# Splitting the transposes of an attention kernel's exponentials into halves of 64 rows

## The chip, the core and the metric

The kernel is one program on one core of a Trainium2 chip. The core has a matrix engine (TensorE, in the profile PE for its matmuls and PEld for the loads of the stationary operand, "weights"), a vector engine (DVE), a scalar engine (ACT), a general engine (GpSimd, POOL) and a queue engine (SP) which here issues DMA transfers. The engines run beside each other and meet at semaphores. Matmuls write into PSUM, eight banks of 128 partitions by 512 float32; DVE and ACT read it from there. The metric is the device time of one execution in microseconds (us); lower is better.

## What is computed

Two decoder layers over 8 sequences of 512 tokens of width 256, all in float32: an attention with relative positions, a feed-forward network with low-rank additions, a second attention, and a mixture of experts. The change lies in the first attention alone, 16 heads of width 16:

```python
scores = jnp.einsum('bhqd,bhkd->bhqk', q, k) / scale
c2p = jnp.take_along_axis(c2p_att, c2p_pos, axis=-1)
p2c = jnp.swapaxes(jnp.take_along_axis(p2c_att, p2c_pos, axis=-1), -1, -2)
scores = scores + (c2p + p2c) / scale
probs = jax.nn.softmax(scores, axis=-1)
ctx = jnp.einsum('bhqk,bhkd->bhqd', probs, v)
```

## The kernel before

The first attention is a loop of 256 steps. A step takes one block of 128 queries (i, one of 4) and two heads (p, one of 2, for the pair within a group of four heads, g) of one sequence (b). It works on the scores of 128 queries by 512 keys, once for each of the two heads. The order of the instructions on each engine is the order in which the program writes them (a schedule by hand); the semaphores are put in where tiles and PSUM banks are shared. What a step n issues, in this order:

- `products`, L363: matmuls of queries by keys into two score banks `sc` (one for each head; there are only two, so the last step's must have been read). Each uses 32 rows of the array. Between its parts stands `strips` for the step five ahead.
- `strips`, L306 to L343: matmuls of 32 rows (`pa`) with the position keys; ACT copies them to SBUF (L313), SP writes them to DRAM (`shift`) and reads them back a row shifted against the next (`winp`, `winc`), and POOL adds a correction (L316, L343). This is how the gather by relative position is made; it gives the DMA engines most of their work.
- `near_keys`, L375: 4 or 6 transposes of 128x128 from `winp`, added onto the score banks.
- `weights`, L389 and L391: DVE adds `winc` to a score bank, writes the result to SBUF as `e` and reduces it to a row bound `low`; ACT takes the exponential in place and sums it.
- `turned`, L394 to L402: the exponentials of the step before, two tiles `e` of 128 queries by 512 keys, are transposed so that keys lie on the partitions. For each tile four transposes of 128x128 fill one bank `et_ps` (L398), and DVE copies the bank to SBUF as `et` (L400). A transpose is a load of the block of `e` as weights, through which an identity streams. There are two such banks, and six tiles `et`.
- `weigh`, L410, in every odd step: 32 matmuls multiply four tiles `et` of two earlier steps by the values. Each loads 16 columns of values and streams 128 columns of `et`, into 32 columns of the array, one strip for each of four heads.
- at most one of a list of other jobs: a projection of queries or keys (`pq`, L282), values (`pv`, L270), the transposes of the normalizer (`spread`, L442), of the normalized input (`pt`, L264), or the output projection (`po`, L455), and with them layer norms on DVE and POOL.

The array is thus used in several shapes in turn: 32 rows (L363, L306), the whole (L375, L398, L282 and the other jobs), and strips of 32 columns (L410).

Of the kernel before, what the change touches and what calls it, by code (L numbers as in the profile page):

```python
# [12 lines left out]
F32 = mybir.dt.float32  # L13
# [8 lines left out]
P = 128  # L22
B, S, H = 8, 512, 256
NT = S // P
# [65 lines left out]
def _l0_attention(nc, tc, a, x, ident, mhalf, carry, prefetch):  # L90
# [6 lines left out]
    with ExitStack() as ctx:  # L97
# [5 lines left out]
        ps_t = pool("a_pst", 2, space=PSUM)  # L103
# [14 lines left out]
        with tc.tile_pool(name="a_pos", bufs=1) as pp:  # L118
# [62 lines left out]
            for n, c in enumerate((P - 1, 0)):  # L181
                f = pp.tile([P, NH, HD], F32, tag=f"end{n}", name=f"end{n}")
# [15 lines left out]
            for (w, name), e0 in (((wq, "bq"), HD), ((wk, "bk"), HD + 2)):  # L198
                for n, f in enumerate(ends):
                    e = e0 + n  # L200
# [8 lines left out]
            for n, (name, e) in enumerate((("bq", HD + 2), ("bq", HD + 3), ("bk", HD), ("bk", HD + 1))):  # L209
# [3 lines left out]
                for g in range(NG):  # L213
                    c = NG * n + g
# [11 lines left out]
        sb = pool("a_sb", 2)  # L226
# [25 lines left out]
        def later(steps, *fs):  # L252
            side.extend((now + steps, f) for f in fs)
# [13 lines left out]
        def values(b, t):  # L267
            pv = misc("pv")
            for k in range(NK):
                nc.tensor.matmul(  # L270
                    pv[:, :H], xnT[:, k, t * P : (t + 1) * P], wv[:, k, :], start=k == 0, stop=k == NK - 1
                )
            nc.vector.tensor_tensor(vs[b % 2][:, t, :], pv[:, :H], rows["bv"], ALU.add)

        def project(b, g):

            sm[b, g] = out = [sb.tile([P, S], F32, tag=f"sm{n}", name=f"sm{n}") for n in range(4)]

            def half(w, n, scale):
                pq = misc("pq")  # L280
                for k in range(NK):
                    nc.tensor.matmul(  # L282
                        pq,
                        w[:, k, 4 * g : 4 * g + 4, :].rearrange("p h e -> p (h e)"),
                        xnT[:, k, :],
                        start=k == 0,
                        stop=k == NK - 1,
                    )
                for m in (n, n + 1):
                    nc.scalar.activation(out[m], pq, AF.Identity, bias=bias[:, m, g : g + 1], scale=scale)  # L290

            return [partial(half, wq, 0, -SCALE), partial(half, wk, 2, 1.0)]
# [98 lines left out]
            nc.scalar.activation(e, e, AF.Exp, bias=low, scale=-1.0, accum_out=totals[b, g][:, i, r : r + 1])  # L391
            return e

        def turned(e):  # L394
            et_ps = ps_t.tile([P, S], F32, tag="pst", name="et_ps")
            for m in range(NT):
                ms = slice(m * P, (m + 1) * P)
                nc.tensor.transpose(et_ps[:, ms], e[:, ms], ident)  # L398
            et = sb.tile([P, S], F32, tag="et", name="et", bufs=6)
            nc.vector.tensor_copy(et, et_ps)  # L400
            return et

        def weigh(n, ets):

            b, g, i, _ = steps[n]
            v = vs[b % 2]
            for m in range(NT):
                for r, et in enumerate(ets):
                    h = 4 * g + r
                    nc.tensor.matmul(  # L410
                        ctx_ps[32 * r : 32 * r + HD, i * P : (i + 1) * P],
                        v[:, m, HD * h : HD * h + HD],
                        et[:, m * P : (m + 1) * P],
                        start=m == 0,
                        stop=m == NT - 1,
                        skip_group_check=True,
                    )
            if i < NT - 1:
                return
            c = sb.tile([P, S], F32, tag="c", name="c", bufs=2)  # L420
            nc.scalar.copy(c, ctx_ps)

            rec = sb.tile([P, NT, 4], F32, tag="rec", name="rec")
            nc.vector.reciprocal(rec, totals.pop((b, g)))
            wide = sb.tile([P, NT, P], F32, tag="wide", name="wide", bufs=1)
            nc.gpsimd.tensor_copy(
                wide.rearrange("p i (r e) -> p i r e", e=32), rec.unsqueeze(3).to_broadcast([P, NT, 4, 32])
            )
            later(3, partial(divide, b, c, wide))
            if g == NG - 1:  # L430
                out, measure, norm = finish(b)
                if b == B - 1:
                    rest.extend([*[partial(out, t) for t in range(NT)], measure, norm])
                else:
                    later(3, *[partial(out, t, misc, sb) for t in range(NT)])
                    later(9, partial(measure, misc, sb))
                    later(12, partial(norm, misc, sb))
# [9 lines left out]
        def finish(b):  # L447

            xn = xns[b % 2]
            stats = []  # L450

            def out(t, bank, pool):
                po = bank("po")
                for g in range(NG):
                    nc.tensor.matmul(  # L455
                        po[:, :H], cns[b][g][:, t * P : (t + 1) * P], wo[:, g, :], start=g == 0, stop=g == NG - 1
                    )
                nc.vector.tensor_tensor(xn[:, t, :], xn[:, t, :], po[:, :H], ALU.add)
                nc.gpsimd.tensor_tensor(xn[:, t, :], xn[:, t, :], rows["bo"], ALU.add)

            def measure(bank, pool):
                stats.extend(_batch_norm_stats(nc, pool, [xn[:, t, :] for t in range(NT)], 1e-7, mhalf))

            def norm(bank, pool):
                for t in range(NT):
                    _normalize(nc, xn[:, t, :], xn[:, t, :], *stats, t)
                    nc.gpsimd.tensor_tensor(xn[:, t, :], xn[:, t, :], rows["ln_scale"], ALU.mult)
                    nc.gpsimd.tensor_tensor(xn[:, t, :], xn[:, t, :], rows["ln_bias"], ALU.add)
                    nc.gpsimd.tensor_tensor(x[b][:, t, :], x[b][:, t, :], xn[:, t, :], ALU.add)

            return out, measure, norm
# [6 lines left out]
        with tc.manual_schedule():  # L478
            for f in [partial(turn, 0, k) for k in range(NK)] + project(0, 0):
                f()  # L480
            for u in range(AHEAD):
                strips(u)
                if u:
                    values(0, u - 1)
            es, ets = None, deque()
            for now in range(len(steps) + 3):
                n = now
                if n < len(steps):
                    b, g, i, p = steps[n]
                    if (i, p) == (0, 0):  # L490
                        totals[b, g] = sb.tile([P, NT, 4], F32, tag="totals", name="totals", bufs=3)
                        if g in (0, NG - 1):
                            while side:
                                side.popleft()[1]()
                        if g + 1 < NG:
                            urgent.extend(project(b, g + 1))
                        elif b + 1 < B:
                            urgent.extend(project(b + 1, 0))
                            later(0, *[partial(values, b + 1, t) for t in range(NT)])
                        if g == NG - 2 and b + 1 < B:  # L500
                            measure, norm = normalized(sb, b + 1)
                            later(1, measure)
                            later(3, norm, *[partial(turn, b + 1, k) for k in range(NK)])
                    scs, parts = products(n)
                    parts.pop(0)()
                    more = parts.pop() if parts else None
                    if n + AHEAD < len(steps):
                        strips(n + AHEAD, more)
                    else:
                        if more is not None:  # L510
                            more()
                        for todo in (reads, adds):
                            if todo:
                                todo.pop(0)()
                    new = []
                    for j in range(2):
                        near_keys(n, j, scs[j])
                        new.append(weights(n, j, scs[j]))
                if n <= len(steps):
                    if es:  # L520
                        ets.extend(turned(e) for e in es)
                    es = new
                if n % 2 and len(ets) >= 4:
                    weigh(n - 3, [ets.popleft() for _ in range(4)])
                if urgent:
                    urgent.popleft()()
                elif side and side[0][0] <= n:
                    side.popleft()[1]()
                for f in prefetch.get(n - len(steps), ()):
                    f(misc, sb)  # L530
            while side:
                side.popleft()[1]()
# [1128 lines left out]
```

## Time and profile before

| What | Value |
|---|---|
| median of 3 runs | 2162.43 us (2162.23 to 2166.1) |
| the profiled execution | 2158.92 us, span 2157.1 us |
| mean granted TensorE clock | 0.962 of full |
| stretch 54 to 600 us: PE, DVE, ACT, POOL busy | 533.5, 378.9, 377.1, 366.0 us; clock 0.99; DMA 0.90, 280 GB/s |
| stretch 600 to 1100 us: the same | 489.3, 347.6, 343.3, 345.9 us; clock 1.00; DMA 0.89, 277 GB/s |
| first and last transpose of L398 | 63.1 and 1149.7 us |
| L398 PEld, weight loads | 2048, 142 ns each, 232.6 us |
| L306 PE / L363 PE / L375 PE busy | 301.6 / 323.0 / 199.7 us |
| L410 PE | 4096, 274 ns each, 137.2 us busy |
| L391 ACT | 512, 716 ns each, 365.9 us |

The span runs from the first instruction to the last and is 1.8 us shorter than the execution's time. "Busy" for PE is the union of pipelined records: a matmul of 273 ns may start every 109, so a busy PE is not one at its peak, and distances between starts tell more than durations. A row of a group gives line, engine, operation, tile written and read, shapes and count; then the busy time in us and the mean in ns of one; then the idle time of the engine just before it and what ended most of it. A row of the timeline gives start and length in us; several like instructions are merged into one row with their count. A row of waits gives who waited for whom, the sum in us, the number of times and the longest.

### The profile page before, as it was taken

The numbers are of one execution on the slowest core, as the hardware profiler recorded it, in microseconds if no ns is written. First come the engines' busy times: TensorE is split into PE (matmuls) and PEld (weight loads), VectorE is DVE, ScalarE is ACT, GpSimd is POOL, SyncE is SP. The second block draws the span as 40 slices with busy tenths as digits, with TensorE's granted clock in tenths as the row PEclk, the third lists the DMA queues.
The fourth block names the chain that finished last, engine by engine and source line by source line (L and its number), as shares of the span: only waits on it lengthen the run. The fifth ranks groups of instructions, "written<-read, shape, count | busy, mean of one in ns | idle before, by whom it ended". The sixth has DMA issues, their size and how long they took to land.

```text
span 2157.1 us, 46358 instructions
## 1 busy us (share of the span) xinstructions
PE 1989.8 (92%) x16100; PEld 1439.5 (67%) x16100; DVE 1401.4 (65%) x3716; ACT 1112.0 (52%) x2382; POOL 1140.5 (53%) x1342
## 2 busy tenths in 40 slices
PE   7999999999999999999998999989988877499997
PEld 4777777777777777767775666645554445388886
DVE  2576676766767677676776655337887776356666
ACT  2776666676666767667662211244444423144443
POOL 4666766767667667676673210112544544355555
PEclk7999999999999999999999999999999987699999
DMA  8998888898898988889893344900111113656888
GB/s 271 317 295 274 273 277 275 277 291 259 265 284 256 296 265 278 281 266 291 266 303 107 100 148 140 122 18 11 46 41 39 51 44 112 248 164 204 260 261 266
DMA packets 389175, 444.50 MB, mean 206 GB/s; under 512 B 43345, under 2 KB 368209, under 8 KB 388945
## 3 DMA queue, kind: packets, MB, share of 16 engines
q1 hardware_dynamic: 374160, 402.20, 61.7%
q0 software_dynamic: 13824, 38.29, 4.8%
q8 instruction: 132, 2.16, 0.4%
q10 hardware_dynamic: 960, 1.05, 0.2%
q14 instruction: 99, 0.80, 0.1%
HBM read 239.26 MB, written 202.19 MB: 205 GB/s over the span
## 4 chain that ended last, share of the span: by engine, by line
PE 27%; DVE 10%; issue 4%; POOL 4%; DMA 3%; ACT 2%; POOLq 0%; DVEq 0%; ACTq 0%; SPq 0%
PE po L665 5%; PE pge L1421 4%; PE ph L657 3%; POOL results L860 2%; PE poe L1439 2%; PE pq L916 2%; PE ao L1006 1%; DVE prod L777 1%; PE po L1035 1%; PE pv L928 1%; DVE value L777 1%; PE ps L953 1%; DVE st L52 1%; DVE xn L62 1%; PE ptr L1413 1%
## 5 line engine op out<-in xcount | busy, mean ns | idle before, releaser
L389 DVE CUSTOM_DVE_ANT_0 e<-sc,winc 128x512 f32<-128x512 f32 x512 | 333.3, 688 | 294.9 <-PE sc L375 133.6
L391 ACT ACTIVATE e<-e,low 128x512 f32<-128x512 f32 x512 | 365.9, 716 | 111.2 <-DVE low L389 105.9
L313 ACT COPY strip<-pa 128x512 f32<-128x512 f32 x512 | 275.3, 591 | 212.7 <-issue 81.3
L316 POOL TENSOR_TENSOR own<-aside,strip 128x512 f32<-128x512 f32 x256 | 268.5, 1049 | 217.5 <-ACT strip L313 198.7
L363 PE MATMUL sc<-sm,sm 32*128 32x256 f32 (+3 forms) x1792 | 323.0, 440 | 15.4 <-DVE low L389 15.4
L400 DVE COPY et<-et_ps 128x512 f32<-128x512 f32 x512 | 328.5, 683 | 0.3 <-PE et_ps L398 0.2
L306 PE MATMUL pa<-pos,sm 32*128 32x256 f32 x2048 | 301.6, 408 | 2.3 <-ACT strip L313 1.3
L398 PE MATMUL et_ps<-ident,e 128*128 128x128 f32 x2048 | 266.4, 273 | 0.2 <-DVE et L400 0.2
L860 POOL DMA_INDIRECT rows<-pay,slot x128 | 141.6, 1106 | 229.5 <-issue 216.3
L363 PEld LDWEIGHTS sc<-sm,sm 32*128 32x128 f32 x1792 | 162.3, 184 | 124.6 <-issue 49.6
L398 PEld LDWEIGHTS et_ps<-ident,e 128*128 128x128 f32 x2048 | 232.6, 142 | 0.6 <-ACT e L391 0.5
L343 POOL TENSOR_TENSOR winp<-winp,own 128x256 f32<-128x256 f32 x256 | 186.5, 728 | 74.8 <-DMA winp<-shift 63.7
L860 POOL DMA_INDIRECT results<-y,r x160 | 155.8, 974 | 122.1 <-ACT y L1441 74.7
L375 PE MATMUL sc<-ident,winp 128*128 128x128 f32 x1280 | 199.7, 285 | 5.3 <-DMA winp<-shift 5.0
L343 POOL TENSOR_TENSOR winc<-winc,own 128x256 f32<-128x256 f32 x256 | 186.6, 729 | 34.1 <-DMA winc<-shift 31.0
L306 PEld LDWEIGHTS pa<-pos,sm 32*128 32x128 f32 x2048 | 180.9, 188 | 15.0 <-ACT strip L313 4.7
L375 PEld LDWEIGHTS sc<-ident,winp 128*128 128x128 f32 x1280 | 136.3, 141 | 81.4 <-issue 63.2
L57 POOL TENSOR_TENSOR rstd<-var,mhalf 128x4 f32<-128x4 f32 x40 | 44.8, 1121 | 252.6 <-DVE var L55 230.6
L1421 PE MATMUL pge<-store,rT 128*128 x640 | 167.9, 385 | 1.1 <-DVE rT L1415 0.5
L410 PE MATMUL ctx_ps<-et,v 128*16 128x128 f32 x4096 | 137.2, 274 | 0.2 <-DVE et L400 0.2
L660 ACT ACTIVATE hT<-ph,b 128x512 f32<-128x512 f32 x64 | 44.0, 687 | 169.8 <-PE ph L657 169.8
L282 PE MATMUL pq<-xnT,wqk 128*128 128x512 f32 x256 | 126.1, 614 | 3.6 <-DVE xnT L77 3.6
(216 smaller groups left out, 3421.4 us busy)
## 6 DMA issues: line engine op xcount, KB each, us to landing
shift<-strip SPq DMA_DIRECT2D x256, 510.0 KB
winp<-shift SPq DMA_DIRECT2D x128, 384.0 KB
winc<-shift SPq DMA_DIRECT2D x128, 384.0 KB
winp<-shift SPq DMA_DIRECT2D x128, 256.0 KB
winc<-shift SPq DMA_DIRECT2D x128, 256.0 KB
rows<-empty SPq DMA_DIRECT2D x8, 2640.0 KB
r<-rows SPq DMA_DIRECT2D x160, 132.0 KB
z<-results SPq DMA_DIRECT2D x32, 512.0 KB
```

Of the source, the lines that this page charges most:

```text
L306: nc.tensor.matmul(pa[:, t * W : (t + 1) * W], src[rs, i * P : (i + 1) * P], pos[rs, g, :], start=True, stop=True)
L313: nc.scalar.copy(st[:, 2 * j : 2 * j + 2, :].rearrange("p t w -> p (t w)"), pas[j])
L316: nc.gpsimd.tensor_tensor(own, aside.unsqueeze(2).to_broadcast([P, 2, 2, P]), st[:, :, W - 1 : W].rearrange("p (j t) o -> p t j o", t=2).t ...
L343: nc.gpsimd.tensor_tensor(dst, dst, own[:, t], ALU.add)
L363: nc.tensor.matmul(sc[:, c0:c1], s[side_][rs, cut : cut + P], s[2 + side_][rs, c0:c1], start=c0 == 0, stop=False, skip_group_check=True,)
L375: nc.tensor.matmul(sc[:, m * P : (m + 1) * P], wins[n + 2 * (m - i)][1][:, j, (i - m + 1) * P : (i - m + 2) * P], ident, start=False, stop ...
L389: nc.vector.tensor_tensor_reduce(e, sc, wins[n][0][:, j, :], 1.0, -LOW, ALU.add, ALU.min, low)
L391: nc.scalar.activation(e, e, AF.Exp, bias=low, scale=-1.0, accum_out=totals[b, g][:, i, r : r + 1])
L398: nc.tensor.transpose(et_ps[:, ms], e[:, ms], ident)
L400: nc.vector.tensor_copy(et, et_ps)
L860: ins = nc.gpsimd.indirect_dma_start(to, bass.IndirectOffsetOnAxis(ap=index, axis=0), source, None, bounds_check=last)
L1421: nc.tensor.matmul(pg[:, :H], rT[:, k * P : (k + 1) * P], w[:, k * H : (k + 1) * H], start=k == 0, stop=k == NK - 1)
```

## The change

Each transpose of a 128x128 block of `e` becomes two: one of the rows 0 to 63 of the array (queries 0 to 63), one of the rows 64 to 127. Each loads a block of 64 rows by 128 columns as weights and streams the 64 columns of the matching quarter of the identity. All blocks of the first half, of both heads, go into one bank and those of the second half into the other. DVE copies each bank into a half of one larger tile `et`, of which there are three in place of six small ones. The weighing streams its 128 columns as two runs of 64 from the two halves.

```diff
-        def turned(e):
-            et_ps = ps_t.tile([P, S], F32, tag="pst", name="et_ps")
-            for m in range(NT):
-                ms = slice(m * P, (m + 1) * P)
-                nc.tensor.transpose(et_ps[:, ms], e[:, ms], ident)
-            et = sb.tile([P, S], F32, tag="et", name="et", bufs=6)
-            nc.vector.tensor_copy(et, et_ps)
-            return et
+        def turned(es):
+            banks = [ps_t.tile([P, S], F32, tag="pst", name="et_ps") for _ in range(2)]
+            for j, e in enumerate(es):
+                for m in range(NT):
+                    for f, bank in enumerate(banks):
+                        rs, c = slice(64 * f, 64 * f + 64), (j * NT + m) * 64
+                        nc.tensor.transpose(bank[:, c : c + 64], e[rs, m * P : (m + 1) * P], ident[rs, rs])
+            et = sb.tile([P, 2, 2, NT, 64], F32, tag="et", name="et", bufs=3)
+            for f, bank in enumerate(banks):
+                nc.vector.tensor_copy(et[:, f].rearrange("p j m q -> p (j m q)"), bank)
+            return [et[:, :, j] for j in range(2)]
...
-                        et[:, m * P : (m + 1) * P],
+                        et[:, :, m, :],
...
-                        ets.extend(turned(e) for e in es)
+                        ets.extend(turned(es))
```

Nothing else is changed: the order of the jobs, the number of copies and of matmuls of every other line are the same.

## The prediction

> **What bounds the kernel now.** I read the page first, for where TensorE is nearly full; then the list of waits over 100 to 1100 us, for who makes it stop; then the timeline of single steps, for what each batch of instructions costs.
>
> ```profile
> PE 1989.8 (92%) x16100; PEld 1439.5 (67%) x16100; DVE 1401.4 (65%) x3716; ACT 1112.0 (52%) x2382; POOL 1140.5 (53%) x1342
> ...
> L389 DVE CUSTOM_DVE_ANT_0 e<-sc,winc 128x512 f32<-128x512 f32 x512 | 333.3, 688 | 294.9 <-PE sc L375 133.6
> ...
> L400 DVE COPY et<-et_ps 128x512 f32<-128x512 f32 x512 | 328.5, 683 | 0.3 <-PE et_ps L398 0.2
> ...
> L398 PE MATMUL et_ps<-ident,e 128*128 128x128 f32 x2048 | 266.4, 273 | 0.2 <-DVE et L400 0.2
> ```
>
> The transposes (L398) run from 63 to 1150 us: 8 in each of 256 steps. The loop takes 4.27 us a step over its steady part. VectorE, ACT and POOL each have idle time there; the waits say what TensorE stops for:
>
> ```profile
> PEld sc L363 <- DVE low L389: 37.8, 96, 1.1
> PEld sc L363 <- DVE et L400: 29.1, 56, 0.8
> ...
> PEld sc L375 <- DMA winp<-shift: 4.2, 9, 0.8
> ```
>
> TensorE stops about once in two steps, at the start of a step (L363), until VectorE has reduced the last score bank (L389) and so freed it. In all other steps it is TensorE's own work that sets the step. Two steps in a row, one without the weighing (L410) and one with it:
>
> ```profile
> 427.25 0.66 PE L375 MATMUL sc<-ident,winp 128*128 128x128 f32 x4
> 427.74 1.04 PE L398 MATMUL et_ps<-ident,e 128*128 128x128 f32 x8
> 428.61 1.88 PE L282 MATMUL pq<-xnT,wqk 128*128 128x512 f32 x4
> ...
> 431.50 0.66 PE L375 MATMUL sc<-ident,winp 128*128 128x128 f32 x4
> 431.99 1.04 PE L398 MATMUL et_ps<-ident,e 128*128 128x128 f32 x8
> 432.96 1.07 PE L410 MATMUL ctx_ps<-et,v 128*16 128x128 f32 x32
> ```
>
> Eight transposes last 1.04 us with a tail of 0.27, so one starts every (1.04-0.27)/7 = 0.11 us. Counted from first weight load to the next group's first load, the group takes 0.87 us when a full-array matmul follows (L282) and 1.07 when the array's shape changes after it (L410, L363): a change of shape costs 0.20 us, of which 0.11 is the last matmul's own streaming and 0.09 a drain.
>
> **What one split transpose costs.** The price depends on whether a block of 128x128 is held up by its weights (a block of e, 128 columns) or by what streams (the identity, 128 columns before, 64 after). Where the shape has just changed, the trace shows the two apart:
>
> ```profile
> 403.19 0.14 PEld L375 LDWEIGHTS sc<-ident,winp 128*128 128x128 f32 x1 [0.33 <-issue]
> ...
> 403.25 0.14 PEld L375 LDWEIGHTS sc<-ident,winp 128*128 128x128 f32 x1
> ...
> 403.36 0.38 PE L375 MATMUL sc<-ident,winp 128*128 128x128 f32 x2
> ```
>
> The second load can begin when the first matmul takes the first set of weights over: 0.06 us. The second matmul follows 0.11 us later. So in a transpose loading takes 60 ns, streaming 128 columns 109, and the load is hidden behind the streaming of the one before. Halving the columns leaves 54 ns of streaming, and 60 ns of loading becomes the limit.
>
> Here two rules of the Trainium skill speak against the change. Its page "TensorE: Matmul & The Clock Gate", section "LDWEIGHTS (loading the stationary operand)", prices a load by columns alone, 128/1.2 = 107 ns, whatever the rows. Then a split block still needs 107 ns and nothing is won. The trace agrees for ordinary loads (two of one row group start at 402.11 and 402.22) but shows 60 for the load of a transpose; I take 60. The same page, section "Part 3: Packing small matmuls", says that a load overlaps matmuls in flight only if their row groups differ: then a row group needs 60+54 = 114 ns a block. The trace has all 128 rows loading while all 128 stream (the next L375 load starts within 2 ns of the matmul before it), so I take max(60,54) = 60.
>
> Whether the two halves run side by side isn't in the trace for 64 rows. The nearest row is four groups of 32 rows:
>
> ```profile
> 402.11 0.19 PEld L363 LDWEIGHTS sc<-sm,sm 32*128 32x128 f32 x2 [0.76 <-issue]
> 402.12 0.19 PEld L306 LDWEIGHTS pa<-pos,sm 32*128 32x128 f32 x2
> ```
>
> Four loads of 0.19 us start within 20 ns, and their matmuls write four banks at once, 7 ns apart. The two halves likewise have disjoint rows and one bank each. Bounds for a block: 54 (only streaming counts) to 120 ns (halves take turns, 2x60). I take 60, plus 7 once for the second half.
>
> **The sum for a step.** New: a change of shape between L375 and the transposes, 0.20. The transposes: 8x0.060 + 0.054 for the last streaming + 0.007 + 0.09 drain = 0.63. Together 0.83 in place of 1.07 or 0.87. So a weighing step gains 0.24 us, a step whose transposes precede a full-array matmul 0.04.
>
> The other edits: VectorE still makes two 128x512 copies of 683 ns a step, now each a half of the queries; the layout of et moves in SBUF, capacity stays 6x512 columns, and L410 streams the same 128 columns as two runs of 64: nothing (no strided stream is in the loop to price it; if it cost 10% it would be 0.1 us per weighing, half the gain). The first copy now waits for all transposes rather than four, but on VectorE it stands behind the two reductions (L389), which end about 1.7 us after the last weight load of L375, when the transposes (0.2+0.6) are over: hidden. The first transposes need both banks free: in the trace the second copy is done at least 0.30 us before the next step's first transpose: hidden. PE issues 16 loads and matmuls more a step, at 7 ns each 0.11 of the 0.6: hidden. No DMA, SP or POOL instruction moves.
>
> **Which steps keep it.** For each step I compared the time when TensorE reaches the next score bank with the end of the reduction that frees it (plus 62 ns, the least seen):
> - Weighing steps, 126: slack is 0.4 us or more in all but some 8. 118x0.24 = 28.3. But in two of them per batch (of 8) VectorE, full with copies and layer-norm statistics, is late in the step after, and its chain starts ahead of the transposes: minus 16x0.24 = 3.8.
> - Steps followed by L282, L270 or L455, 60: slack 0.4 to 1.1. 60x0.04 = 2.4.
> - Steps followed by nothing, by L442 or by L264, about 69: TensorE waits for VectorE in the next step or just makes it: 0.
> - The last ten steps hang on DMA (the chain of waits there is shift, winp, winp, shift from 1101 to 1134): minus 1.4.
>
> 28.3-3.8+2.4-1.4 = 25.5 us. **What is late next** is DMA: it is 0.90 busy (280 GB/s) in the loop, and POOL waits 53 us in all for the windows (winp). After the stretch in each batch where POOL does the layer norm, reads lag, and TensorE already stops 0.2 to 0.7 us for a window some 12 steps on. Those 12 steps hold 6 weighing steps, about 1.5 us of gain, of which I give back some 40%: 0.6x8 = 5. As a share the demand only rises to 0.92, and from 75 to 109 us the engines carried 0.99, so throughput isn't the wall. Gain 25.5-5 = 20.5, rounded to 21: the profiled run's 2158.9 becomes 2138. The median of the runs shown is 3.5 us above that execution, so 2141 for the median.
>
> **Rivals.**
> 1. *The halves don't run side by side, or the load isn't hidden* (slower). With x for a block, a weighing step gains 0.72-8x, an even one 0.52-8x; summed over the steps where TensorE decides, it turns at x = 0.08 us. At 0.109 (load priced by columns), over the 102 weighing steps that count and the 60 even ones with 23 of the L442 steps that just make it: 102x0.15 + 83x0.35 = 44 lost, 2206; at 0.120: 102x0.24 + 83x0.44 = 61, 2223. For: no 64-row transpose is in the trace. Against: the four 32-row loads, the 60 ns load. Chance 0.16.
> 2. *DVE and DMA take it all.* The waits at L363 and for winp grow by what the transposes lose; what stays is under 4 us: about 2160. For: 82 us of TensorE's stops are for VectorE already (37.8 and 29.1 on its load side, 15.4 on its matmul side), DMA at 0.90. Against: 118 of the 126 weighing steps have 0.4 us of slack, more than 0.24. Chance 0.05.
> 3. *The load is cheaper for half the rows*, x = 0.054: 0.05 more in 102+60 steps, 8 us: 2133. Inside the forecast's spread.
>
> **Numbers.** Faster 0.79 (forecast with rival 3), no change 0.05, slower 0.16. No change means within 0.2%, 4.3 us, about what a measurement of this kernel can tell. Of the forecast's own spread: all of DMA's share kept and x = 0.054 give 2162-34 = 2128; half of the 25.5 lost gives 2150; a drain twice as long (0.09 more in 180 steps, 16 us) 2157. The range 2124 to 2159 holds nearly all of the forecast; the slower cases stay outside.
>
> **What would show it.** Right: 4096 transposes in pairs a few ns apart, pairs 0.06 us apart; L398's group of a weighing step 0.63 us long after a stop of 0.2 on the load engine; TensorE's wait for the reduction up in unweighed steps; steps with a weighing and projection 0.24 shorter. Wrong: pairs 0.11 or more apart, or starts alternating at 0.06 (rival 1); weighing steps shorter, but waits on winp longer by as much (rival 2); L410's group over 1.0 us (the strided stream).

## The result and the profile after

The changed kernel takes 2157.37 us in the median of 20 runs (2149.47 to 2165.1), the kernel before 2163.16 on the same chip: ratio 0.9969, 95% interval 0.9957 to 0.9981. By the ratio it is faster by some 6.7 us (the medians differ by 5.8), a third of the forecast's 21. The profiled execution has a span of 2155.4 us. These are its rows for those shown of before, from the page (columns as there):

```profile
PE 1969.2 (91%) x18148; PEld 1374.6 (64%) x18148; DVE 1402.5 (65%) x3716; ACT 1110.9 (52%) x2382; POOL 1141.3 (53%) x1342
...
L389 DVE CUSTOM_DVE_ANT_0 e<-sc,winc 128x512 f32<-128x512 f32 x512 | 333.4, 688 | 290.7 <-PE sc L375 135.3
...
L405 DVE COPY et<-et_ps 128x512 f32<-128x512 f32 x512 | 328.5, 683 | 2.4 <-PE et_ps L402 2.4
...
L402 PE MATMUL et_ps<-ident,e 64*128 64x64 f32 x4096 | 186.9, 232 | 0.7 <-DVE et L405 0.7
L402 PEld LDWEIGHTS et_ps<-ident,e 64*128 64x128 f32 x4096 | 151.3, 141 | 45.1 <-issue 22.1
```

The transposes are now L402. VectorE does what it did, and waits for the transposes 2.4 us in all. Busy time of the transposes falls from 266 to 187 us, but the idle time of the load engine before them is new: 45 us, or 0.18 us a step. That is the change of shape.

The waits over 100 to 1100 us:

```profile
PEld sc L363 <- DVE low L389: 49.4, 112, 1.5
PEld sc L363 <- DVE et L405: 28.4, 50, 0.8
...
PEld sc L375 <- DMA winp<-shift: 10.4, 15, 2.2
```

The wait for the reduction and that for `winp` have both grown, from 37.8 and 4.2 us. Two steps in a row in detail, the loads of the first from the timeline of the load engine, then the second from that of the matmuls:

```profile
426.59 0.42 PEld L375 LDWEIGHTS sc<-ident,winp 128*128 128x128 f32 x4 [0.33 <-issue]
427.18 0.58 PEld L402 LDWEIGHTS et_ps<-ident,e 64*128 64x128 f32 x16 [0.17 <-issue]
...
430.82 0.33 PE L375 MATMUL sc<-ident,winp 128*128 128x128 f32 x1
431.39 0.55 PE L375 MATMUL sc<-ident,winp 128*128 128x128 f32 x3 [0.25 <-DMA winp<-shift]
431.87 0.71 PE L402 MATMUL et_ps<-ident,e 64*128 64x64 f32 x16
432.51 1.07 PE L415 MATMUL ctx_ps<-et,v 128*16 128x128 f32 x32
```

The sixteen loads come in eight pairs; 0.58 less the 0.14 of the last load, over seven, is 0.063 us a pair. From the start at 431.87 to that of the weighing at 432.51 the group takes 0.64 us. The group of L375 ahead of it, where it does not wait, is 0.20 us longer than before: 0.59 from its first load at 426.59 to that of L402 at 427.18, where the kernel before has 0.39. So the step's own arithmetic holds: predicted were 0.060, 0.63 and 0.20. The row at 431.39 shows the other thing: in the middle of L375 TensorE waits for its data, `winp`.

What no step predicted is in the clock. The view of stretches gives start, end and length; then the busy time of PE, PEld, DVE, ACT and POOL, each with its number of instructions; and in its last columns the granted clock, the DMA share and the rate in GB/s. Four stretches of 3.4 us, 136.5 us apart, with half the clock, and as the last row the same place of a later batch, with the full clock:

```profile
141.50:144.90 3.40, 3.40 (x50) 2.69 (x52) 2.64 (x6) 2.48 (x6) 2.30 (x3) 0.50 0.57 181
278.00:281.40 3.40, 3.40 (x50) 2.69 (x52) 2.62 (x6) 2.52 (x7) 2.26 (x3) 0.50 0.60 190
414.60:418.00 3.40, 3.40 (x45) 2.77 (x46) 2.21 (x7) 2.79 (x7) 1.98 (x3) 0.50 0.56 184
551.20:554.60 3.40, 3.40 (x50) 2.73 (x52) 2.50 (x6) 2.52 (x7) 2.27 (x3) 0.51 0.55 174
686.00:689.40 3.40, 3.40 (x67) 2.61 (x64) 2.80 (x8) 3.25 (x9) 1.43 (x2) 1.00 0.55 185
```

For 3.4 us TensorE's clock is halved; such a stretch is called a window of the clock, or a halved window, from here on. Between 75 and 1095 us there are 7 such windows: five in the 22nd step of a batch of 32, where VectorE has just done a layer norm, one in a 14th and one in a first step. The kernel before has one. The stretches just ahead of three of those above show what comes before it; the last row lies 136.5 us behind the third, and no halved window follows it:

```profile
138.10:141.50 3.40, 2.47 (x22) 1.44 (x21) 3.18 (x7) 2.00 (x6) 2.03 (x3) 1.00 0.87 275
274.60:278.00 3.40, 2.47 (x21) 1.40 (x20) 3.22 (x7) 1.96 (x6) 2.07 (x3) 1.00 0.87 259
547.70:551.10 3.40, 2.48 (x21) 1.37 (x20) 3.31 (x7) 1.86 (x5) 2.16 (x3) 1.00 0.83 259
684.20:687.60 3.40, 3.04 (x29) 2.01 (x31) 2.80 (x8) 2.73 (x7) 1.32 (x2) 1.00 0.88 263
```

VectorE is busy nearly all the time, and TensorE, which waits for it, does fewer matmuls ahead of the halved windows than in the last row. What a window costs in the 22nd step can be read in this one profile, from that step in two batches, by the timeline of the matmuls:

```profile
277.75 1.31 PE L375 MATMUL sc<-ident,winp 128*128 128x128 f32 x6
278.99 1.11 PE L402 MATMUL et_ps<-ident,e 64*128 64x64 f32 x16
280.03 1.73 PE L415 MATMUL ctx_ps<-et,v 128*16 128x128 f32 x32
281.69 0.66 PE L264 MATMUL pt<-ident,xn 128*128 128x128 f32 x4
...
686.57 0.87 PE L375 MATMUL sc<-ident,winp 128*128 128x128 f32 x6
687.38 0.72 PE L402 MATMUL et_ps<-ident,e 64*128 64x64 f32 x16
688.02 1.07 PE L415 MATMUL ctx_ps<-et,v 128*16 128x128 f32 x32
689.02 0.66 PE L264 MATMUL pt<-ident,xn 128*128 128x128 f32 x4
```

From the start of L375 to that of L264 it is 3.94 us with the halved clock and 2.45 without: 1.5 us for a window in this step.

### The profile page after: what moved, and what is told of

The parts are those of the page before. It is cut to its first block, busy times and chain, and to the rows that moved or that the text cites. A ratio compares the mean times of both kernels' runs of the same rounds, so it can differ in the third digit from the quotient of the medians.

```text
span 2155.4 us, 49995 instructions
## 1 busy us (share of the span) xinstructions
PE 1969.2 (91%) x18148; PEld 1374.6 (64%) x18148; DVE 1402.5 (65%) x3716; ACT 1110.9 (52%) x2382; POOL 1141.3 (53%) x1342
## 4 chain that ended last, share of the span: by engine, by line
PE 34%; DVE 12%; issue 3%; DMA 3%; ACT 2%; POOL 2%; SPq 0%; POOLq 0%; DVEq 0%; ACTq 0%
PE pge L1426 6%; PE po L670 5%; PE poe L1444 3%; PE ph L662 3%; PE pq L921 2%; PE ptr L1418 2%; DVE prod L782 1%; PE ao L1011 1%; PE sc L363 1%; PE pv L933 1%; DVE value L782 1%; PE po L1040 1%; DVE st L52 1%; DMA winp<-shift 1%; DVE xn L62 1%
## 5 line engine op out<-in xcount | busy, mean ns | idle before, releaser
L375 PE MATMUL sc<-ident,winp 128*128 128x128 f32 x1280 | 205.5, 290 | 9.9 <-DMA winp<-shift 9.9
L375 PEld LDWEIGHTS sc<-ident,winp 128*128 128x128 f32 x1280 | 139.7, 144 | 87.0 <-issue 59.5
L402 PE MATMUL et_ps<-ident,e 64*128 64x64 f32 x4096 | 186.9, 232 | 0.7 <-DVE et L405 0.7
L402 PEld LDWEIGHTS et_ps<-ident,e 64*128 64x128 f32 x4096 | 151.3, 141 | 45.1 <-issue 22.1
L415 PE MATMUL ctx_ps<-et,v 128*16 128x128 f32 x4096 | 141.0, 279 | 1.0 <-DVE et L405 1.0
```

The costliest lines, as they stand in the source:

```text
L375: nc.tensor.matmul(sc[:, m * P : (m + 1) * P], wins[n + 2 * (m - i)][1][:, j, (i - m + 1) * P : (i - m + 2) * P], ident, start=False, stop ...
L402: nc.tensor.transpose(bank[:, c : c + 64], e[rs, m * P : (m + 1) * P], ident[rs, rs])
```

## The experiments

Two theories stood against each other. **Clock**: the faster transposes leave TensorE so idle in the layer norms' steps, where it waits for VectorE, that its clock is halved there, and it loses what it gained elsewhere. **DMA**: the data read back as `winp` can't come faster, and the waits at L375 take the gain.

The later stages, the same code in all kernels, took 1005 to 1028 us from the end of the attention on (1005.3 in the profile of before, 1010.1 of after, 1027.5 of e6), and the times of before lay between 2160 and 2174 us from session to session. So times are compared by ratios of one session, and the attention by its steps 8 to 239, from first load to first load in one profile each. Across sessions even ratios differ: the same kernel gave 0.9886 in one and 0.9915 in another (e7, e14), so a difference of 0.003 between rows of two sessions says nothing. One session each are e1 to e4; e5 to e8; e9 to e11; and e12 to e15. In the table "filled" stands for repeated transposes and "norms in halves" for the layer norms issued in smaller pieces; both are described below it.

| Kernel | Ratio (interval) | Steps 8 to 239, us | Halved windows, 75 to 1095 us | Waits at L375, us |
|---|---|---|---|---|
| before | 1 | 995.0 | 1 | 5.3 |
| changed | 0.9969 (0.9957 to 0.9981) | 986.3 | 7 | 15.8 |
| changed, e5 | 0.9974 (0.9960 to 0.9987) | 981.6 | 6 | 16.6 |
| changed, e12 | 0.9976 (0.9966 to 0.9986) | 989.3 | 12 | 21.8 |
| filled, e1 | 0.9947 (0.9928 to 0.9966) | 977.0 | 0 | 10.7 |
| filled, e13 | 0.9932 (0.9910 to 0.9954) | 981.9 | 1 | 14.6 |
| before, filled, e9 | 1.0001 (0.9989 to 1.0012) | 995.1 | 0 | 5.6 |
| before, norms in halves, e7 | 0.9886 (0.9866 to 0.9905) | 972.5 | 1 | 3.5 |
| the same, e14 | 0.9915 (0.9897 to 0.9933) | 973.3 | 1 | 5.1 |
| changed, norms in halves, e8 | 0.9885 (0.9864 to 0.9907) | 962.7 | 2 | 12.1 |
| the same, filled, e10 | 0.9854 (0.9832 to 0.9875) | 959.1 | 2 | 7.7 |
| the same, e15 | 0.9862 (0.9845 to 0.9880) | 963.8 | 2 | 13.9 |

"Waits at L375" is what its groups last beyond 0.06 us and 0.109 for each further load, and, in kernels with the split, beyond 0.20 for the new change of shape. In a halved window the group is longer too, by 0.4 to 0.7 us, so part of that column is clock. Of the experiments outside the table, e2, e4 and e6 have 1 halved window each, e3 has 8.

**Repeated transposes (e1; e9 as control on the kernel before).** The split transposes of five steps of a batch are done twice, with the same values, where TensorE waits for VectorE:

```diff
-            for j, e in enumerate(es):
+            for again in range(2 if now % 32 in (12, 14, 18, 19, 20) else 1):
+                for j, e in enumerate(es):
```

> The changed kernel, with the split transposes of five steps of each batch (12, 14, 18, 19, 20 of its 32, where TensorE waits for VectorE's layer norms) done twice over, with the same values. Clock theory: in those stretches the faster transposes leave TensorE idle enough for the clock gate to halve its clock (6 more windows of 3.4 us in the loop than before, about 1.5 us lost at each). The repeated transposes lie in waits and keep it busy: the halved windows at 141, 278, 415, 551 us go, and the kernel is about 9 us faster than the changed one, 2148 us, ratio to the kernel before about 0.993. DMA theory: what was lost are the waits for winp at L375 (19 us against 9); repeated transposes change nothing in them: 2157 us, or slower by the work added.

> The kernel before, with its whole transposes of the same five steps of each batch done twice: the control of the filled kernel. Clock theory: the kernel before has hardly a halved window in the loop (1 up to 1095 us), so there is nothing to win, and each repeat costs 0.87 us of which the waits cover 0.5 to 0.8: 2 to 5 us slower, ratio 1.001 to 1.002. If repeated transposes help for another reason than the clock, it gains as the changed kernel did, ratio about 0.997.

More work made the changed kernel faster, though by less than expected (0.9947, not 0.993), and the interval of that ratio still overlaps the changed kernel's; e12 and e13 below settle it in one session. No halved window is left in e1; the step that took 6.2 us in five of seven batches takes 4.71 or 4.72 in all seven:

```profile
545.76 0.88 PE L375 MATMUL sc<-ident,winp 128*128 128x128 f32 x6
546.57 0.71 PE L403 MATMUL et_ps<-ident,e 64*128 64x64 f32 x16
547.22 1.07 PE L416 MATMUL ctx_ps<-et,v 128*16 128x128 f32 x32
548.21 0.66 PE L264 MATMUL pt<-ident,xn 128*128 128x128 f32 x4
```

This is the step at the same place as the slow one at 551 us of the changed kernel. On the kernel before, the repeats change nothing (1.0001; expected was a loss of 2 to 5 us, so the waits covered it): without the split, where only one window was to be won back, they don't help.

**Fewer bytes (e2, e3, e4).** Every second step's read of `winc` is left out; the scores of those steps lack that term:

```diff
-                for t, dst in ((1, wk_[:, :, c0:c1]), (0, wc[:, :, lo * P : hi * P])):
+                for t, dst in ((1, wk_[:, :, c0:c1]), (0, wc[:, :, lo * P : hi * P]))[: 2 - p]:
```

> The kernel before with every second step's read of winc left out (a quarter of the DMA bytes of the loop, so that half of the scores lack one of their terms). DMA theory: waits at L375 of 9 us go, 2163 becomes about 2154, and this is the base for the next run. Clock theory: the same base, since it has nothing to say here; at most 9 us faster.

> The changed kernel with the same reads of winc left out. DMA theory: with the waits for windows gone the split keeps its 25 us against the light kernel before: ratio to the kernel before about 0.984, 2129 us. Clock theory: it keeps its halved windows after the layer norms, the gain over the light kernel before stays at about 12 us or less: 2142 us or more.

> Both: reads of winc left out and transposes repeated in five steps of a batch. If both causes are at work: about 25 us under the light kernel before, 2129 us, and clearly under each of the two runs that have only one of them. DMA theory alone: the same as the light changed kernel. Clock theory alone: the same distance to the light changed kernel as the filled one has to the changed one, 9 us.

The share was misjudged there: a step moves 510 KB of writes and twice 256 or 384 KB of reads, so half of the reads of `winc` are a seventh of 1150 KB, not a quarter. Measured against one and the same before: 0.9990 (0.9980 to 1.0001), 0.9924 (0.9903 to 0.9945), 0.9906 (0.9886 to 0.9926). The waits at L375 hardly fall: 4.4 us in e2, 14.7 in e3, 11.2 in e4, beside 5.3, 15.8 and 10.7 with all bytes. So they are not for the engines' throughput. The light changed kernel still has 8 halved windows and gains 14 us on the light kernel before, more than the changed kernel on before and less than 25: it supports neither theory alone. The repeats take it from 8 halved windows to 1, but win only 3.3 us (2150.98 to 2147.68, with overlapping intervals; 3.4 us in steps 8 to 239), where the clock theory expected 9.

**The changed kernel again (e5), and the halves in turn (e6).** In e6 all blocks of the first half come first, then all of the second:

```diff
-            for j, e in enumerate(es):
-                for m in range(NT):
-                    for f, bank in enumerate(banks):
+            for f, bank in enumerate(banks):
+                for j, e in enumerate(es):
+                    for m in range(NT):
```

> The changed kernel itself, to have it beside the next runs on one chip and to see in a second profile whether the halved clock windows recur. Clock theory: again 5 or more windows of 3.4 us at half clock between 75 and 1100 us, about 136.5 us apart, each in the stretch of the layer norms; ratio to the kernel before 0.996 to 0.998. DMA theory has no reason for such windows to recur at one place of a batch.

> The changed kernel with the order of the split transposes turned: all sixteen... that is, all 8 of the first half, then all 8 of the second, so that the two halves don't alternate. If it is the alternation that lets the halves run side by side, 16 blocks follow each other at 60 ns, the group of transposes lasts 0.2 + 16x0.06 + 0.15 = 1.3 us in place of 0.83, and 180 steps lose 0.48 us each; less what waits for DMA and the clock give back (10 to 20 us): 2220 us, ratio 1.03. If the halves overlap whatever the order, nothing changes: 2157 us.

e5 has its halved windows again, 6 in five places, but not 136.5 us apart as expected, and in the 14th step of a batch more often (four) than in the 22nd (two in a row): both steps follow a layer norm (there are two in a batch). e6 is slower, 1.0113 (1.0094 to 1.0132), but by less than 1.03; it has 1 halved window. The alternation matters; yet without it the group of transposes lasts 0.95 us in the median, not the 1.1 that sixteen blocks of 0.06 and a tail of 0.15 would take, because the second half doesn't wait for the end of the first. The timeline of the load engine in e6:

```profile
433.02 0.88 PEld L402 LDWEIGHTS et_ps<-ident,e 64*128 64x128 f32 x16 [0.17 <-issue]
```

Sixteen loads one after the other at 0.062 would end 0.93+0.14 after the first; they end after 0.88. Load by load the trace has two interleaved runs of loads 0.06 us apart from 433.32 on. A record does not say which half it is of, but by this spacing the second half begins there, when two or three of the first half's loads are still to come.

**The layer norms in halves (e7, e8).** The statistics and the normalizing are issued two tiles at a time, over four steps in place of two, on both kernels:

```diff
-                    later(9, partial(measure, misc, sb))
-                    later(12, partial(norm, misc, sb))
+                    later(9, *[partial(measure, misc, sb, part) for part in range(2)])
+                    later(11, *[partial(norm, misc, sb, part) for part in range(2)])
...
-                            later(1, measure)
-                            later(3, norm, *[partial(turn, b + 1, k) for k in range(NK)])
+                            later(1, *[partial(measure, part) for part in range(2)])
+                            later(3, *[partial(norm, part) for part in range(2)], *[partial(turn, b + 1, k) for k in range(NK)])
```

> The kernel before with the two layer norms of each batch, statistics and normalizing, issued in halves over four steps each in place of whole in two. VectorE then no longer holds up the score banks for 2 to 3 us in one step. Clock theory: the kernel before loses little to the clock (2 windows); it gains what TensorE waits for VectorE in these steps, 2 us a batch, 15 us: 2148 us, ratio 0.993. DMA theory: the windows read late stay late, nothing gained: ratio 1.000.

> The changed kernel with the layer norms in halves. Clock theory: no stretch is left in which TensorE idles for a window's length, the halved windows after the layer norms go, and the split keeps its 20 to 25 us against the spread kernel before: ratio to the kernel before 0.982 to 0.985, 2127 us. DMA theory: the gap to the spread kernel before stays at the 7 us seen for the change alone, and the waits at L375 stay near 19 us.

The kernel before gains more than expected, 0.9886: waits that I had taken as fixed were worth 22 us in the steps. In e8 only 2 halved windows are left and the steps gain 10 us on e7 in the profiles, but the times are equal (0.9885), where the clock theory expected 0.982 to 0.985. Of those 10 us the profiled executions keep 4: in e8 the last steps and the later stages took longer (1024.2 against 1019.9 us from the end of the attention on). What the split alone is worth on top of e7 is thus not shown.

**Both (e10), and reading early (e11).** e11 takes e8 and reads `winp` and `winc` back right behind their own write:

```diff
-            if len(reads) > 1:
+            while reads:
                 reads.pop(0)()
```

> The changed kernel with the layer norms in halves and the repeated transposes. Clock theory: with the layer norms in halves only 2 halved windows were left in the loop, so repeats win nothing more, 0 to 2 us: ratio to the kernel before 0.987 to 0.989. If the repeats win 5 us again, the clock was not what they mended.

> The changed kernel with the layer norms in halves, and each window read back right behind its own write on SP's queue, not behind the write of the next step. Leaving out a quarter of the bytes did not shorten the waits for winp at L375 (12 us over steps 8 to 239 in the spread kernel), so they are waits for a chain write, read, correction that starts a fixed number of steps ahead; reading up to 1.5 us earlier in long steps should take half of them: 5 us faster than the spread kernel, ratio 0.986. But SP then sits behind each landing, and in short steps the next write starts up to 1 us late: if that rules, no gain or slower.

e10 is the fastest version, 2128.9 us, ratio 0.9854 (0.9832 to 0.9875). Against the expectation it lies under e8, by 0.0031 in the ratio and with 959.1 against 962.7 us in the steps, though both have two halved windows; the waits at L375 are 4.4 us shorter. By the expectation's own test the repeats may then mend something besides the clock. The two ratios are of different sessions and their intervals overlap, so that stays open. e11 is slower by far, 1.2058. Its waits, the first row from the SP queue's own list:

```profile
SPq L352 <- DMA shift<-strip: 1125.8, 256, 9.1
```

SP issues in order, so it stood 4.4 us behind each of 256 landings and the next write could not start. In the order of before, each read behind the next step's write, most of that landing is hidden.

**The two comparisons that were open, on one chip (e12 to e15).**

> The changed kernel, for comparison on the chip of the next three. Clock theory: 5 or more halved windows between 75 and 1095 us in its profile, ratio to the kernel before 0.996 to 0.998.

> The filled kernel again. Clock theory: no or one halved window in the loop, 5 to 9 us under the changed kernel, ratio 0.993 to 0.995. If the earlier difference of 0.2% was chance of chip and session, the two ratios are equal.

> The kernel before with the layer norms in halves, again: ratio 0.988 to 0.989.

> The changed kernel with both, again. Clock theory: the split with its clock kept is worth, above the spread kernel before, the 11 us by which the attention ended earlier in their profiles (1107 against 1118 us): ratio about 0.983 to 0.985. If the split is worth nothing once VectorE no longer holds TensorE up, the ratio is that of the run before this.

The filled kernel is 9.4 us under the changed one (2153.63 against 2163.01), and the intervals of their ratios are apart. The changed kernel has 12 halved windows here, the filled one has 1. On top of the norms in halves the split and the repeats together are worth 10.0 us (2138.45 against 2148.46), and these intervals are apart as well. The two ratios themselves, 0.9915 and 0.9862, missed their expectations of 0.988 to 0.989 and 0.983 to 0.985.

**What a window costs.** It depends on the step that it falls in. Two steps later, and against the same steps of other batches of the same profile, a single window in the 22nd step has cost 1.4 to 1.7 us (changed kernel, e12, e3), one in the 14th only 0.3 to 1.0 (the same and e5): there the 16th step begins with a wait of 1.30 us for VectorE when the clock is full, and this wait shrinks to 0.6 us or none behind a halved window. For the changed kernel that sums to five times 1.5, one of 0.3 and one of 1.3 (3.3 in a first step, less a stop of 2.0 there for data of `winp`): 9.1 us. In e12 and in e3 five of the windows fall in a 14th step, and in e5 four of its six, so their number alone says little: 11 windows more than in e13 cost e12 9.4 us, 7 more than in e4 cost e3 3.3.

## Why the prediction was wrong

**The cost of a split transpose: right.** Sixty nanoseconds a pair, the halves side by side, load hidden behind streaming: 0.063 measured. (The loop's own pace, given as 4.27 us a step, is 995.0/232 = 4.29; nothing hangs on it.) The Trainium skill's price by columns (107 ns) and its rule that a load overlaps only matmuls of other row groups would both have made the change a loss; the rows of the trace decided rightly. e6 shows that the alternation in program order is part of it: without it the group lasts 0.30 us longer, and the steps 0.13 on average (1017.3 against 986.3 us for 232). The strided stream of L410 (now L415) costs nothing: 273 ns a matmul in the median, 1.00 us a group, as before.

**The sum for a step: right.** In the medians a weighing step without another job went from 4.14 to 3.91 us, one with a projection from 5.45 to 5.24, an unweighed one with a projection from 4.25 to 4.22; forecast were 0.24, 0.24 and 0.04 less.

**The steps that keep it: the step that failed.** The prediction said of the 69 steps in which "TensorE waits for VectorE in the next step or just makes it: 0". It took the waiting as free. But the waits had brought TensorE near the point where its clock is halved: with faster transposes it idles more in the layer norms' steps, and in the step behind them it runs at half the clock for a window, at 1.5 us in the 22nd step of a batch. The 7 windows come to 9 us. That is the difference between the changed kernel and the filled e1 over steps 8 to 239 (986.3 and 977.0; e13 has 981.9), and e12 against e13 has 9.4 us in the times. The clock does not appear among the prediction's rivals at all, though the profile of before had a halved window in the loop (in the 22nd step of a batch) as a warning:

```profile
554.30:557.70 3.40, 3.40 (x24) 2.70 (x18) 1.93 (x5) 2.48 (x6) 0.94 (x1) 0.50 0.16 54
```

The Trainium skill has it on the page quoted for the load, "TensorE: Matmul & The Clock Gate", section "Part 1: The HAM clock gate (the "warmup" mystery)": the clock is set by how busy the array was in a free-running window of 3.4 us. This case agrees. The windows last 3.41 us, and the seven starts lie 40, 40, 40, 69, 24 and 27 times that apart. Forty windows, 136.5 us, are also the length of the batches there (136.1 to 136.9), so that the same step was hit batch after batch until a shorter one (134.0) shifted it. How idle a window must be can be estimated from the traces: counting 0.109 us for 128 columns from each matmul's start, TensorE streamed for 0.25 to 0.53 of the window ahead of 43 of the 44 halved ones of all profiles but e11's (the 44th follows a halved one), and so little in only 26 of the 4726 others between 75 and 1095 us. Windows so idle number 10 to 16 in the three profiles of the changed kernel, 1 in that of the kernel before, 0 and 1 in e1 and e13. It is no sharp limit: some of the 26 idled as long as those ahead of halved ones, in e11 windows with up to 0.66 were followed by a halved one, and some records of matmuls may be missing.

**What is late next: right in kind, somewhat small.** For DMA 5 us were given back. In the filled kernels, with the clock kept, waits at L375 rose from 5.3 to 10.7 and 14.6 us, so 5 to 9. That its share of 0.90 wasn't the wall held: a seventh fewer bytes left the waits nearly as they were. That they come from a chain of write, read and correction begun a fixed number of steps ahead is argued only; e11, meant to shorten it, held up the queue instead.

With the clock kept the forecast comes nearer: e1 gains 18.0 us over 232 of the 256 steps in its profile, e13 13.1, and by their ratios, 0.9947 and 0.9932, the whole kernel gains 11 to 15 of the 21. Of the rest, part is the larger wait for `winp` and part the last steps: in the changed kernel the gain since step 8 falls from 8.7 us at step 240 to 6.2 at step 254. What is left is not accounted for; the later stages alone differ by more between profiles.

**Rivals.** The slower one (halves in turn) didn't come; its price was set too high too, 0.120 a block where e6 has (0.95-0.15)/8 = 0.10. The second (DVE and DMA take it all) came in part: the waits for `winp` took 5 to 9 us, and the clock, which it didn't name, about 9.

## What to carry to other kernels

A wait of TensorE is not free if it leaves the array idle enough for its clock to be halved. Before counting a saved matmul in a waiting stretch as nothing, look at the granted clock there, and price a halved window by the step that it would hit (here 0.3 to 1.5 us). If a change makes TensorE idler in such a stretch, remove the wait (here the layer norms issued in smaller pieces, worth 18 to 25 us on the kernel before) or fill it with repeated work (9.4 us on the changed one). In float32, splitting transposes by rows paid here because the weights load faster (0.06 us) than 128 columns stream (0.109), and only with the halves alternating in program order: e6, without that, is slower than the kernel before.

## What the runs showed of the hardware

Behind a change of shape, the second load of 128 columns follows the first after 0.06 us in float32 transposes (403.19 and 403.25 of before) and after 0.11 in ordinary float32 matmuls (402.11 and 402.22). Loads of one row group can overtake those of another that stand ahead of them in the program (e6, as read from their spacing). Repeated transposes kept the clock up (7 halved windows without them, none in e1; 12 in e12, 1 in e13), so transposes count as activity. By the estimate above, TensorE had streamed for 0.53 or less of the 3.41 us ahead of 43 of 44 halved windows; it needn't have stood still. And one in-order DMA queue that waits for each landing, 4.4 us in the mean, cost 20% of this kernel (e11).
